# The adapters of the last four batches multiplied together in four column quadrants

## The chip, the cores and the metric

The kernel runs on one core of a Trainium2 chip. The metric is the device time of one execution in microseconds; the figure given for a kernel is the median of several runs. The profile is of one further execution, taken by the hardware profiler, and has its own time.

A core has four engines that matter here, each with its own instruction stream: TensorE multiplies matrices (PE in the profile, PEld for its loads of weights), VectorE (DVE) and ScalarE (ACT) work elementwise, and SyncE (SP) issues nearly all the transfers. TensorE writes to PSUM, which has eight banks of 128 partitions by 512 fp32 numbers.

## The reference

Eight batches of 256 tokens with 1,024 features each go through a low-rank adapter that each batch chooses by its number, then through a feed-forward layer in quantized form, and the result is added to the input. Cut to what matters (one matmul each; `q` rounds to fp8 after division by an input scale):

```
B_sel, A_sel = B[ids], A[ids]              # per batch: 16 x 1024 and 1024 x 16
Bx   = einsum('bni,bri->bnr', x, B_sel)    # "B product", rank 16
c    = einsum('bnr,bor->bno', Bx, A_sel)   # "A product"
gate = q(c) @ gate_w.T ;  up = q(c) @ up_w.T       # 1024 -> 2752
hid  = silu(gate) * up
out  = x + q(hid) @ down_w.T                       # 2752 -> 1024
```

The adapters are applied in fp32, the feed-forward layer takes the fp8 values of its inputs.

## The kernel before, in words

The tokens are transposed on the host, so features lie on partitions and tokens are columns. The 2,048 tokens are four tiles of 512 columns, t = 0 to 3; tile t holds batches 2t and 2t+1 as two halves of 256 columns. The 1,024 features are eight slices of 128, k = 0 to 7. The 2,752 inner features are 22 chunks c of 128 (the last is a half).

**Adapters.** For each t, `load_adapters` reads the two chosen adapters: `b_sel[t]` (128 rows of 136 numbers for each batch: eight slices of 16 columns, and eight scales) and `a_sel[t]` (64 rows for each batch). `spread_b(t)` (L397) copies each 16-column slice of B four times side by side on VectorE (L401), so that a slice is 64 columns wide. `times_b(t)` (L406) multiplies: for each k, one matmul for each of the two batches, 64 columns of weights against 256 columns of x, the first batch into PSUM partitions 0 to 63 and the second into 64 to 127 (L412). Because B stands there four times, the rank-16 result of each batch appears at four places, at partitions 0, 32, 64 and 96, each pair of which belongs to one batch. VectorE copies it to `bm` (L420). `times_a(t)` (L423) then multiplies by A from those four places at once, each a matmul with 16 rows, for different output slices (L430): two halves of eight matmuls, each into four PSUM banks `c`, which ScalarE and VectorE in turn round to fp8 into `xg[t]` (L446, L442).

**Gate and up.** `gate_up(c, t)` (L449) multiplies one chunk of weights by one tile: eight matmuls of 128x128 by 512 columns into y0 (gate) and eight into y1 (up) (L457), in the order of slices `ORDER`, in which `times_a` gets them ready. ScalarE applies silu to y0 (L470), VectorE multiplies by y1 into `hid` (L471). For some (c, t), ScalarE also runs notes (L384, L391): passes over weights, `xg` and `hid` that sum up low bits and squares, from which the kernel decides at its end whether its fast path was allowed.

**Down.** For each output slice, 22 matmuls for each tile (L553), then VectorE adds x (L561), and the result is written out.

**Order.** The order of work is written out by hand at L493 to L516, TensorE follows it. Tile 0's adapter comes first. Then, for t = 1, 2, 3: the B product of tile t, chunk 0 of tile t-1 (for t > 1), chunk 1 of tile t-1, in whose middle (between y0 and y1) stands the A product of tile t. After tile 3: chunks 0 and 1 of it, then chunks 2 to 21 over all tiles. PSUM is one pool of eight banks that all of these take in turn.

**Transfers.** SyncE issues them in program order: x and adapters of tile 0, weights of chunk 0, adapters and x of tile 1, chunk 1, adapters and x of tile 2, the same of tile 3, and then chunk 2 and on. Weights have five buffers, so chunks 0 to 4 are loaded without waiting for a buffer; the load of a later chunk waits until a former one has been multiplied and noted. The transfers take turns on eight completion semaphores, so that each also waits for the landing of the eighth transfer before it. An adapter's place in memory comes from a register that SyncE loads from the list of numbers (L307).

Of the kernel before, what the change touches and what calls it, by code (L numbers as in the profile page):

```python
# [8 lines left out]
F32 = mybir.dt.float32  # L9
# [4 lines left out]
AF = mybir.ActivationFunctionType  # L14
ALU = mybir.AluOpType
AX = mybir.AxisListType

P = 128
T = 2048
SEQ = 256  # L20
NB = 8
H = 1024
I = 2752
R = 16
NH = H // P
NI = (I + P - 1) // P
TAIL = I - (NI - 1) * P
TB = 512
NTB = T // TB
HALF = NI // 2  # L30

ORDER = [0, 1, 4, 5, 2, 3, 6, 7]
# [4 lines left out]
GATE_IN, GATE_W, UP_IN, UP_W, DOWN_IN, DOWN_W = range(6)  # L37
# [214 lines left out]
def adaln_ffn(  # L252
# [13 lines left out]
    nc = tc.nc  # L266
    const = ctx.enter_context(tc.tile_pool(name="const", bufs=1))
    psum = ctx.enter_context(
        tc.tile_pool(name="psum", bufs=8, space=bass.MemoryType.PSUM)
    )  # L270


    ids_i = const.tile([1, NB], I32, name="ids_i")
# [13 lines left out]
    with ExitStack() as fast:  # L287
        acts = fast.enter_context(tc.tile_pool(name="acts", bufs=1))
        lora = fast.enter_context(tc.tile_pool(name="lora", bufs=1))
# [4 lines left out]
        xs = [acts.tile([P, NH, TB], F32, name=f"x{t}") for t in range(NTB)]  # L294
        xg = [acts.tile([P, NH, TB], FP8, name=f"xg{t}") for t in range(NTB)]
# [1 line left out]

        b_sel = [lora.tile([P, 2, NH * R + 8], F32, name=f"b_sel{t}") for t in range(NTB)]  # L300
        a_sel = [lora.tile([P, H // 2], F32, name=f"a_sel{t}") for t in range(NTB)]

        def load_adapters(t, *queues):

            for queue in queues:
                ids_t = [
                    queue.value_load(ids_i[0:1, b : b + 1], min_val=0, max_val=7)  # L307
                    for b in (2 * t, 2 * t + 1)
                ]
                for j, i in enumerate(ids_t):  # L310
                    if queue is queues[0]:
                        queue.dma_start(out=b_sel[t][:, j], in_=b8[bass.ds(i * P, P), :])  # L312
                    if queue is queues[-1]:
                        queue.dma_start(
                            out=a_sel[t][64 * j : 64 * (j + 1)],
                            in_=a8[bass.ds(i * 64, 64), :],
                        )

        def load_x(t, first, n):
            ks = slice(first, first + n)  # L320
            nc.sync.dma_start(out=xs[t][:, ks, :], in_=x4[t][:, ks, :])
# [3 lines left out]
        def load_gate_up(c):  # L325
            n = NH if c == NI - 1 else 2 * NH
            w = wpool.tile([P, 2 * NH, P], F32, tag="w", name="w_gu")[:, :n]
            at = c * 2 * NH * P
            nc.sync.dma_start(
                out=w, in_=w_gu[:, at : at + n * P].rearrange("p (k n) -> p k n", n=P)  # L330
            )
            w_of[c] = w
# [3 lines left out]
        load_adapters(0, nc.scalar, nc.sync)  # L336
        load_x(0, 6, 2)
        load_gate_up(0)
        for t in range(1, NTB):
            load_adapters(t, nc.sync)  # L340
            load_x(t, 0, 4)
            load_x(t, 4, 4)
            if t == 1:
                load_gate_up(1)


        sc = b_sel[0][:, 0, NH * R :]
        inv = const.tile([P, 6], F32, name="inv")
# [48 lines left out]
        def spread_b(t):  # L397
            b_pad = lora.tile([P, 2, NH, 4, R], F32, tag="b_pad", name="b_pad", bufs=2)
            for j in range(2):
                b = b_sel[t][:, j, : NH * R].rearrange("p (k o r) -> p k o r", k=NH, o=1)  # L400
                spread = nc.vector.tensor_copy(b_pad[:, j], b.to_broadcast((P, NH, 4, R)))  # L401
                if t:
                    tc.keep_in_program_order(spread)
            return b_pad

        def times_b(t, b_pad):  # L406


            bx = psum.tile([P, SEQ], F32, tag="ps", name="bx")
            for k in range(NH):  # L410
                for j in range(2):
                    nc.tensor.matmul(  # L412
                        bx[64 * j : 64 * (j + 1)],
                        lhsT=b_pad[:, j, k].rearrange("p o r -> p (o r)"),
                        rhs=xs[t][:, k, bass.ts(j, SEQ)],
                        start=(k == 0),
                        stop=(k == NH - 1),
                    )
            bm = lora.tile([P, SEQ], F32, tag="bm", name="bm", bufs=2)
            nc.vector.tensor_copy(bm, bx)  # L420
            return bm

        def times_a(t, bm):  # L423

            for half in range(2):
                cs = [psum.tile([P, 2, SEQ], F32, tag="ps", name=f"c{q}") for q in range(4)]
                for i in range(2):
                    for q in range(4):
                        rows = slice(32 * q, 32 * q + R)
                        nc.tensor.matmul(  # L430
                            cs[q][:, i],
                            lhsT=a_sel[t][rows, bass.ts(2 * half + i, P)],
                            rhs=bm[rows],
                            start=True,
                            stop=True,
                        )
                for q in range(4):
                    k = 4 * (q % 2) + 2 * half
                    to = xg[t][:, k : k + 2, bass.ts(q // 2, SEQ)]
                    scale = inv[:, GATE_IN : GATE_IN + 1]  # L440
                    if q % 2:
                        nc.vector.tensor_scalar(  # L442
                            to, cs[q], scale, None, ALU.mult, saturate=False
                        )
                    else:
                        nc.scalar.activation(to, cs[q], AF.Copy, scale=scale, saturate=False)  # L446


        def gate_up(c, t, between=None):  # L449
            tail = c == NI - 1  # L450
            w = w_of[c]
            cols = bass.ts(t, TB)
            ys = []
            for j in range(1 if tail else 2):
                y = psum.tile([P, TB], F32, tag="ps", name=f"y{j}")
                for k in ORDER:
                    nc.tensor.matmul(  # L457
                        y,
                        lhsT=high(w[:, j * NH + k, :]),
                        rhs=xg[t][:, k, :],  # L460
                        start=(k == ORDER[0]),
                        stop=(k == ORDER[-1]),
                    )
                ys.append(y)
                if between and not j:
                    between()
            gates, ups = (ys[0], ys[-1]) if not tail else (ys[0][:TAIL], ys[0][TAIL:])
            rows = slice(TAIL, P) if tail else slice(0, P)
            g = work.tile([P, TB], F32, tag="g", name="g")
            nc.scalar.activation(g[rows], gates, AF.Silu, scale=gate_s[: gates.shape[0]])  # L470
            nc.vector.scalar_tensor_tensor(  # L471
                hid[c][rows, cols],
                in0=ups,
                scalar=up_by_down[rows],
                in1=g[rows],
                op0=ALU.mult,
                op1=ALU.mult,
                saturate=False,
            )
            if t == 1 and c > 1:  # L480
                for done in {2: (0, 2), 3: (1, 3)}.get(c, (c,)):
                    note_low_bits(w_of[done], P, done)
                if c <= 1 + 2 * NTB:
                    i, half = divmod(c - 2, 2)
                    ks = slice(half * NH // 2, (half + 1) * NH // 2)
                    note_squares(xg[i][:, ks, :], P, c - 2)
                for done in (0, 1) if c == 2 else (c - 1,):
                    note_squares(hid[done], P, 2 * NTB + done)
# [9 lines left out]
        b_pad = spread_b(0)  # L498
        times_a(0, times_b(0, b_pad))
        b_pad = spread_b(1)  # L500
        gate_up(0, 0)
        for t in range(1, NTB):
            bm = times_b(t, b_pad)
            if t > 1:
                gate_up(0, t - 1)
            if t + 1 < NTB:
                b_pad = spread_b(t + 1)
            gate_up(1, t - 1, between=lambda: times_a(t, bm))
        gate_up(0, NTB - 1)
        gate_up(1, NTB - 1)  # L510
        for c in range(2, NI):
            load_gate_up(c)
            if c == NI - 2:
                nc.sync.dma_start(out=wt[TAIL:], in_=w_d_tail)
            for t in range(NTB):
                gate_up(c, t)  # L516
# [20 lines left out]
        for k in range(NH):  # L537
# [10 lines left out]
            for t in range(NTB):  # L548
                cols = bass.ts(t, TB)
                y = psum.tile([P, TB], F32, tag="ps", name="yd")  # L550
                for c in range(NI):
# [3 lines left out]
                        lhsT=high(wt[:, k, :] if tail else ws[c]),  # L555
                        rhs=hid[c][:, cols],
                        start=(c == 0),
                        stop=tail,
# [9 lines left out]
    with tc.If(others > 0):  # L568
        general(
            tc, psum, x4, aT, bT, w_gu, w_d, w_d_tail, outT, ids,  # L570
            inv=inv, gate_s=gate_s, up_by_down=up_by_down, down_s=down_s,
# [76 lines left out]
```

## Time and profile before

| | us |
|---|---|
| median of 3 runs | 491.61 |
| lowest, highest | 491.53, 492.59 |
| the profiled execution's own time | 492.39 |
| its span, first to last instruction | 490.5 |
| PE busy | 481.2 |
| ACT busy | 192.1 |
| DVE busy | 106.8 |
| matmuls of the B products (L412), busy in all | 15.0 |
| matmuls of the A products (L430), busy in all | 8.0 |

A line of a group reads: line, engine, operation, what it writes and reads, shapes, how often, then busy time in all and mean nanoseconds of one, and the idle time of the engine just before it with what ended that. Matmuls overlap in the array, so one's length times their number is more than the busy time. In the chain of work that ended last, each piece has its start, its length, engine, tile, line and the number of instructions; in the lines of SyncE, the length is that of issuing, not of the transfer.

### The profile page before, as it was taken

The page shows a single profiled execution, that of the slowest core. Times are in us where ns is not written, and L with a number is a line of the kernel's source. Part 1 is how long each engine was busy: PE and PEld are TensorE (multiplying, and loading weights), DVE is VectorE, ACT ScalarE, POOL GpSimd, SP SyncE. Part 2 cuts the span into 40 slices and gives each one's busy share as a digit, 9 for nine tenths or more (in the row PEclk, how much of TensorE's full clock was granted, in tenths as well). Part 3 has the DMA queues.
Part 4 walks back from the last instruction along what each step waited for, and adds up shares of the span by engine and source line. Part 5 has one row for each costly group of instructions (what it writes and reads, how often), then busy time and mean ns, then how long its engine had stood idle before and what let it go on. Part 6 is the DMA issues. An engine that isn't in the chain of part 4 may idle for free.

```text
span 490.5 us, 5796 instructions
## 1 busy us (share of the span) xinstructions
PE 481.2 (98%) x2416; PEld 226.4 (46%) x2416; DVE 106.8 (22%) x163; ACT 192.1 (39%) x243; POOL 2.9 (1%) x6
## 2 busy tenths in 40 slices
PE   8999999999999999999999999999999999999995
PEld 7455544444444444444444444444444444444442
DVE  1344412222121212222121212132111111112111
ACT  1222358756666554444545454459212112021000
POOL 2000000000000000000000000000000000000000
PEclk9899999999999999999999999999999999999998
DMA  8996014422112222222112111112515425333111
GB/s 290 351 373 255 1 38 142 165 86 87 37 55 80 86 87 86 87 86 84 36 53 86 43 61 53 60 54 82 166 71 160 135 86 176 106 115 119 43 66 49
DMA packets 13284, 52.66 MB, mean 107 GB/s; under 512 B 1538, under 2 KB 2562, under 8 KB 9666
## 3 DMA queue, kind: packets, MB, share of 16 engines
q1 hardware_dynamic: 12960, 52.07, 31.0%
q8 instruction: 21, 0.34, 0.3%
q10 hardware_dynamic: 290, 0.14, 0.1%
q14 instruction: 13, 0.11, 0.1%
HBM read 43.81 MB, written 8.39 MB: 106 GB/s over the span
## 4 chain that ended last, share of the span: by engine, by line
PE 97%; DMA 1%; ACT 0%; DVE 0%; ACTq 0%; issue 0%
PE y L457 61%; PE yd L553 31%; PE bx L412 3%; PE c L430 1%; DMA b_sel<-b 1%; ACT xg L446 0%; ACT L275 0%; DVE o L561 0%; ACTq L307 0%; ACTq L274 0%; DVE bm L420 0%; DVE b_pad L401 0%; DVE inv L349 0%; PE count L531 0%; ACTq L312 0%
## 5 line engine op out<-in xcount | busy, mean ns | idle before, releaser
L457 PE MATMUL y<-xg,w_gu 128*128 128x512 fp8e4 x1376 | 299.9, 381 | 0.5 <-ACT xg L446 0.5
L457 PEld LDWEIGHTS <-w_gu 128*128 128x128 bf16 x1376 | 134.5, 98 | 164.9 <-issue 5.2
L553 PE MATMUL yd<-hid,w_d 128*128 128x512 fp8e4 x672 | 150.3, 379 | 0.0
L470 ACT ACTIVATE g<-y,gate_s 128x512 f32<-128x512 f32 (+1 forms) x88 | 59.8, 681 | 152.4 <-PE y L457 152.4
L471 DVE SCALAR_TENSOR_TENSOR hid<-y,up_by_down,g 128x512 fp8e4<-128x512 f32 (+1 forms) x88 | 66.0, 751 | 226.3 <-PE y L457 157.5
L553 PEld LDWEIGHTS <-w_d 128*128 128x128 bf16 x672 | 65.7, 98 | 79.1
L384 ACT ACTIVATE junk<-w_d 128x1408 bf16<-128x1408 uint16 (+1 forms) x16 | 21.2, 1324 | 89.3 <-DMA w_d<-w_d 89.1
L561 DVE SCALAR_TENSOR_TENSOR o<-yd,down_s,x 128x512 f32<-128x512 f32 x32 | 24.0, 751 | 121.9 <-PE yd L553 121.9
L391 ACT ACTIVATE junk<-hid 128x2048 bf16<-128x2048 fp8e4 x22 | 41.9, 1906 | 0.5
L384 ACT ACTIVATE junk<-w_gu 128x2048 bf16<-128x2048 uint16 (+1 forms) x22 | 41.0, 1863 | 0.1
L412 PE MATMUL bx<-x,b_pad 128*64 128x256 f32 x128 | 15.0, 382 | 1.4 <-DVE b_pad L401 1.4
L391 ACT ACTIVATE junk<-xg 128x2048 bf16<-128x2048 fp8e4 x8 | 15.3, 1907 | 0.2
L446 ACT ACTIVATE xg<-c,inv 128x512 fp8e4<-128x512 f32 x16 | 9.7, 687 | 13.5 <-PE c L430 13.5
L412 PEld LDWEIGHTS bx<-x,b_pad 128*64 128x64 f32 x128 | 10.0, 137 | 6.1 <-DVE b_pad L401 1.7
L442 DVE TENSOR_SCALAR xg<-c,inv 128x512 fp8e4<-128x512 f32 x16 | 10.9, 745 | 6.4 <-PE c L430 6.4
L553 PE MATMUL yd<-hid,w_dt 128*128 128x512 fp8e4 x32 | 12.1, 379 | 0.0
L430 PE MATMUL c<-bm,a_sel 16*128 16x256 f32 x128 | 8.0, 387 | 0.5 <-DVE bm L420 0.5
L495 PE MATMUL warm<-zeros 128*128 128x128 bf16 x78 | 6.9, 277 | 1.0 <-DVE zeros L277 1.0
L430 PEld LDWEIGHTS c<-bm,a_sel 16*128 16x128 f32 x128 | 6.2, 184 | 2.5 <-DVE bm L420 1.0
L495 PEld LDWEIGHTS <-zeros 128*128 128x128 bf16 x78 | 6.8, 130 | 1.0 <-DVE zeros L277 1.0
L553 PEld LDWEIGHTS <-w_dt 128*128 128x128 bf16 x32 | 3.1, 98 | 3.8
L420 DVE COPY bm<-bx 128x256 f32<-128x256 f32 x4 | 1.7, 425 | 12.1 <-PE bx L412 12.1
(31 smaller groups left out, 24.0 us busy)
## 6 DMA issues: line engine op xcount, KB each, us to landing
w_gu<-w_gu SPq DMA_DIRECT2D x21, 1024.0 KB, 4.8
outT<-o SPq DMA_DIRECT2D x32, 256.0 KB, 2.1
x<-x SPq DMA_DIRECT2D x7, 1024.0 KB, 9.8
w_d<-w_d SPq DMA_DIRECT2D x8, 704.0 KB, 4.6
w_d<-w_d SPq DMA_DIRECT2D x8, 640.0 KB, 3.8
x<-x SPq DMA_DIRECT2D x2, 512.0 KB, 6.4
a_sel<-a SPq DMA_DIRECT2D x8, 128.0 KB, 7.0
w_gu<-w_gu SPq DMA_DIRECT2D x1, 512.0 KB
```

The costliest lines, as they stand in the source:

```text
L384: nc.scalar.activation(junk_like(w), low(w), AF.Copy, accum_out=lows[:rows, column : column + 1])
L391: nc.scalar.activation(junk_like(q), q, AF.Square, accum_out=squares[:rows, column : column + 1])
L412: nc.tensor.matmul(bx[64 * j : 64 * (j + 1)], lhsT=b_pad[:, j, k].rearrange("p o r -> p (o r)"), rhs=xs[t][:, k, bass.ts(j, SEQ)], start=( ...
L430: nc.tensor.matmul(cs[q][:, i], lhsT=a_sel[t][rows, bass.ts(2 * half + i, P)], rhs=bm[rows], start=True, stop=True,)
L442: nc.vector.tensor_scalar(to, cs[q], scale, None, ALU.mult, saturate=False)
L446: nc.scalar.activation(to, cs[q], AF.Copy, scale=scale, saturate=False)
L457: nc.tensor.matmul(y, lhsT=high(w[:, j * NH + k, :]), rhs=xg[t][:, k, :], start=(k == ORDER[0]), stop=(k == ORDER[-1]),)
L470: nc.scalar.activation(g[rows], gates, AF.Silu, scale=gate_s[: gates.shape[0]])
L471: nc.vector.scalar_tensor_tensor(hid[c][rows, cols], in0=ups, scalar=up_by_down[rows], in1=g[rows], op0=ALU.mult, op1=ALU.mult, saturate=F ...
L495: nc.tensor.matmul(warm[:, :P], lhsT=zeros, rhs=zeros, start=(i == 0), stop=(i == 77))
L553: nc.tensor.matmul(y, lhsT=high(wt[:, k, :] if tail else ws[c]), rhs=hid[c][:, cols], start=(c == 0), stop=tail,)
L561: nc.vector.scalar_tensor_tensor(o, in0=y, scalar=down_s, in1=xs[t][:, k, :], op0=ALU.mult, op1=ALU.add)
```

## The change

Tiles 0 and 1 stay as they are. For tiles 2 and 3, that is batches 4 to 7:

- `load_four` reads the four adapters, B without copies: `b_four` holds the four batches' B side by side, with 16 zero columns after the last (a memset), and `a_four` the four A, at partitions 0, 32, 64 and 96, 16 rows each, over all 1,024 outputs. It stands after chunk 1's weights in the order of transfers; then come x of tiles 2 and 3, and then chunk 2.
- `four_times_b` multiplies, for each k, all four batches, each with 32 columns of `b_four` (its 16, and the 16 that follow, whose results nobody reads) into its own quadrant of 32 PSUM partitions. `bm` then holds the four batches' results at partitions 0, 32, 64 and 96.
- `four_times_a` multiplies by A, one batch for each quadrant of rows, two output slices at a time.
- The order of work changes: both chunks 0 and 1 of tile 1 are done before the B product of the four, chunk 2 of tile 0 lies around the first half of the A product, chunk 2 of tile 1 after the second half, and then chunks 0, 1 and 2 of tile 2 and of tile 3. From chunk 3 on it is as before. Tiles 2 and 3 take the slices in plain order.
- The notes of chunk 2 move from tile 1 to tile 3.

```diff
+        b_four = lora.tile([P, 4 * (NH * R + 8) + R], F32, name="b_four")
+        nc.vector.memset(b_four[:, 4 * (NH * R + 8) :], 0.0)
+        a_four = lora.tile([P, H], F32, name="a_four")
...
+        def load_four():
+            for q in range(4):
+                i = nc.sync.value_load(ids_i[0:1, 4 + q : 5 + q], min_val=0, max_val=7)
+                nc.sync.dma_start(
+                    out=b_four[:, q * (NH * R + 8) : (q + 1) * (NH * R + 8)],
+                    in_=b8[bass.ds(i * P, P), :],
+                )
+                nc.sync.dma_start(
+                    out=a_four[32 * q : 32 * q + R], in_=aT[bass.ds(i * R, R), :]
+                )
...
-        for t in range(1, NTB):
-            load_adapters(t, nc.sync)
+        load_adapters(1, nc.sync)
+        load_x(1, 0, 4)
+        load_x(1, 4, 4)
+        load_gate_up(1)
+        load_four()
+        for t in (2, 3):
             load_x(t, 0, 4)
             load_x(t, 4, 4)
-            if t == 1:
-                load_gate_up(1)
+        load_gate_up(2)
...
+        def four_times_b():
+
+            bx = psum.tile([P, SEQ], F32, tag="ps", name="bx")
+            for k in range(NH):
+                for q in range(4):
+                    at = q * (NH * R + 8) + k * R
+                    nc.tensor.matmul(
+                        bx[32 * q : 32 * (q + 1)],
+                        lhsT=b_four[:, at : at + 32],
+                        rhs=xs[2 + q // 2][:, k, bass.ts(q % 2, SEQ)],
+                        start=(k == 0),
+                        stop=(k == NH - 1),
+                    )
+            bm = lora.tile([P, SEQ], F32, tag="bm", name="bm", bufs=2)
+            nc.vector.tensor_copy(bm, bx)
+            return bm
+
+        def four_times_a(bm, pairs):
+            for i in pairs:
+                cs = [psum.tile([P, 2, SEQ], F32, tag="ps", name=f"c{q}") for q in range(4)]
+                for k in range(2):
+                    for q in range(4):
+                        rows = slice(32 * q, 32 * q + R)
+                        nc.tensor.matmul(
+                            cs[q][:, k],
+                            lhsT=a_four[rows, bass.ts(2 * i + k, P)],
+                            rhs=bm[rows],
+                            start=True,
+                            stop=True,
+                        )
+                for q in range(4):
+                    to = xg[2 + q // 2][:, 2 * i : 2 * i + 2, bass.ts(q % 2, SEQ)]
+                    round_to(to, cs[q], nc.vector if q % 2 else nc.scalar)
...
-                for k in ORDER:
+                order = ORDER if t < 2 else range(NH)
+                for k in order:
...
-            if t == 1 and c > 1:
+            if c > 1 and t == (NTB - 1 if c == 2 else 1):
...
-        for t in range(1, NTB):
-            bm = times_b(t, b_pad)
-            if t > 1:
-                gate_up(0, t - 1)
-            if t + 1 < NTB:
-                b_pad = spread_b(t + 1)
-            gate_up(1, t - 1, between=lambda: times_a(t, bm))
-        gate_up(0, NTB - 1)
-        gate_up(1, NTB - 1)
-        for c in range(2, NI):
+        bm = times_b(1, b_pad)
+        gate_up(1, 0, between=lambda: times_a(1, bm))
+        gate_up(0, 1)
+        gate_up(1, 1)
+        bm = four_times_b()
+        gate_up(2, 0, between=lambda: four_times_a(bm, (0, 1)))
+        four_times_a(bm, (2, 3))
+        gate_up(2, 1)
+        for t in (2, 3):
+            for c in range(3):
+                gate_up(c, t)
+        for c in range(3, NI):
             load_gate_up(c)
...
```

More of the change, by code (lines that the diff above doesn't have):

```diff
@@ L296, in adaln_ffn @@
         hid = [acts.tile([P, T], FP8, name=f"hid{c}") for c in range(NI)]
-        b_sel = [lora.tile([P, 2, NH * R + 8], F32, name=f"b_sel{t}") for t in range(NTB)]
-        a_sel = [lora.tile([P, H // 2], F32, name=f"a_sel{t}") for t in range(NTB)]
+        b_sel = [lora.tile([P, 2, NH * R + 8], F32, name=f"b_sel{t}") for t in range(2)]
+        a_sel = [lora.tile([P, H // 2], F32, name=f"a_sel{t}") for t in range(2)]
+        b_four = lora.tile([P, 4 * (NH * R + 8) + R], F32, name="b_four")
+        nc.vector.memset(b_four[:, 4 * (NH * R + 8) :], 0.0)
+        a_four = lora.tile([P, H], F32, name="a_four")
         def load_adapters(t, *queues):
@@ L421, in times_b, with round_to @@
             return bm
+        def round_to(to, c, engine):
+            scale = inv[:, GATE_IN : GATE_IN + 1]
+            if engine is nc.vector:
+                nc.vector.tensor_scalar(to, c, scale, None, ALU.mult, saturate=False)
+            else:
+                nc.scalar.activation(to, c, AF.Copy, scale=scale, saturate=False)
         def times_a(t, bm):
@@ L439, in times_a @@
                     to = xg[t][:, k : k + 2, bass.ts(q // 2, SEQ)]
[L440 to L443, printed above, removed]
-                        )
-                    else:
-                        nc.scalar.activation(to, cs[q], AF.Copy, scale=scale, saturate=False)
+                    round_to(to, cs[q], nc.vector if q % 2 else nc.scalar)
[26 more added lines that the diff above has]
+                            stop=True,
+                        )
+                for q in range(4):
+                    to = xg[2 + q // 2][:, 2 * i : 2 * i + 2, bass.ts(q % 2, SEQ)]
+                    round_to(to, cs[q], nc.vector if q % 2 else nc.scalar)
         def gate_up(c, t, between=None):
@@ L460, in gate_up @@
                         rhs=xg[t][:, k, :],
-                        start=(k == ORDER[0]),
-                        stop=(k == ORDER[-1]),
+                        start=(k == order[0]),
+                        stop=(k == order[-1]),
                     )
```

## The prediction

> **What bounds the kernel now.** I read the page's totals and chain first, then its groups, then the chain in order of time, then the waits, and last the queue of SyncE.
>
> Page of the kernel before: span, totals, the chain's shares, three groups.
>
> ```profile
> span 490.5 us, 5796 instructions
> ...
> PE 481.2 (98%) x2416; PEld 226.4 (46%) x2416; DVE 106.8 (22%) x163; ACT 192.1 (39%) x243; POOL 2.9 (1%) x6
> ...
> PE 97%; DMA 1%; ACT 0%; DVE 0%; ACTq 0%; issue 0%
> ...
> L457 PE MATMUL y<-xg,w_gu 128*128 128x512 fp8e4 x1376 | 299.9, 381 | 0.5 <-ACT xg L446 0.5
> ...
> L412 PE MATMUL bx<-x,b_pad 128*64 128x256 f32 x128 | 15.0, 382 | 1.4 <-DVE b_pad L401 1.4
> ...
> L430 PE MATMUL c<-bm,a_sel 16*128 16x256 f32 x128 | 8.0, 387 | 0.5 <-DVE bm L420 0.5
> ```
>
> TensorE is the chain for 97% of the span. So a microsecond taken from its stream after the start comes off the end, if no new wait takes its place. The groups say how the matmuls overlap: each lasts about 380 ns, but y (L457) takes 299.9 / 1376 = 218 ns apiece, bx 15.0 / 128 = 117 ns and c 8.0 / 128 = 62 ns. The trace's single start times give the pattern: y one every 216 ns, bx two 7 ns apart every 216 ns, c four 7 ns apart every 216 ns. I call one such beat a round: bx now runs two wide (two halves of the columns), c four wide (four row quadrants). Each fp32 product stands in the trace as two passes, so the 16 products of one `times_b` are 32 passes, or 16 rounds.
>
> Chain in order of time: start, length, what.
>
> ```profile
> 27.08 1.94 PE c L430 x32
> 29.02 1.83 PE y L457 x8
> 30.85 3.60 PE bx L412 x32
> 34.46 5.29 PE y L457 x24
> 39.74 1.94 PE c L430 x32
> 41.68 1.83 PE y L457 x8
> 43.52 3.60 PE bx L412 x32
> 47.12 5.29 PE y L457 x24
> 52.41 1.94 PE c L430 x32
> 54.35 278.10 PE y L457 x1288
> ```
>
> The adapters of t=1 to 3 lie on the chain bare, between runs of y. No gap stands between the pieces, and TensorE's waits hold only four entries, all before 16.4 us. After that it never waits.
>
> **What the Trainium skill says.** "TensorE: Matmul & The Clock Gate", Part 3 (Measured speedup vs the span model): tiles of the array run together, span about one matmul's length plus 4 ns per further tile, and 16 tiles of 32x32 gave 10.6x, thus four column tiles over each row strip at once. The trace agrees for two column tiles (7 ns apart) and four row tiles; it shows no four column tiles over all 128 rows. "TensorEngine Tiling (Array Packing)", Key Properties: changing the tiling mode drains the engine. The trace prices it: the step into or out of a block is 0.31 us instead of 0.216. "DMA: Bandwidth & Descriptors", How many engines (k): a transfer is split by its outer rows, so 16 rows go to 16 engines; no row shows that here.
>
> **The change, part by part.**
>
> *B products of t=2, 3.* Before, one block costs, from the last y before it to the first y after it less one y beat, 34.389 - 30.473 - 0.216 = 3.70 us, and 0.01 more in the next beat: 3.71. It is made of the step in 0.309, a first round of 0.267, 14 further rounds of 0.216, and the step out 0.312. Two blocks: 7.42. After: `four_times_b` has 32 products = 64 passes, four wide 16 rounds, so the same block once; four weight loads in its first round may make that 0.320, as in c. I take 3.74. Gain 3.68 us. The same number of passes is issued; what goes is 16 rounds and one pair of steps.
> Bounds of the width, which this trace does not show: four wide 3.72 to 3.78; two wide 64/2 = 32 rounds, 3.71 + 16 x 0.216 = 7.17; one at a time 64 rounds, 14.1. I take four wide: c shows that four matmuls with their loads are issued within one beat, bx that loads of different columns over the same rows overlap, and the page named above has four column tiles together.
>
> *A products.* Before two blocks `times_a` (t=2, 3) of 32 passes, (41.615 - 39.364) - 0.216 + 0.01 = 2.05 each. After two blocks `four_times_a` of 32 passes, four row quadrants. Same: 0.
>
> *PSUM under the A products.* Now block, 8 y, block follow at once. Eight banks turn in order. From the row before, with block start = 0: ACT empties its c from 1.16 to 3.58, DVE from 1.20 to 3.93, then hid to 4.70. Block two starts at 3.77 and needs the second to fifth c, free by 3.0. Its last c, at about 4.75, needs the bank of y1, freed by hid at 4.70. I put 0 to 0.15 for that, 0.03 taken.
>
> *Spreading copies and the added memset.* Four copies of 0.42 us (L401, t=2, 3) go, one small memset comes, on DVE, which is 22% busy and idle from 1.1 to 8.4 us: 0. Without that cover the memset would cost what DVE's first ones last, 0.06 to 0.11 us; the copies were hidden too.
>
> *Order of y.* The number of y matmuls is the same. `ORDER` for t=2, 3 becomes plain, since the pairs are emptied in that order. The last part of their xg is written about 4 us after the second A block starts; that block (2 us) and the y of (2,1) (3.45 us) stand before the first reader: 0. Without that cover, the first y of (0,2) would wait up to 2 us.
>
> *DMA.* SyncE issues in program order, and the DMAs take eight semaphores in turn, so each waits for the eighth before it.
>
> ```profile
> 17.14 1.49 SPq L321 DMA_DIRECT2D x<-x  x2
> 20.73 0.34 SPq L312 DMA_DIRECT2D b_sel<-b  x1
> 24.07 0.47 SPq L314 DMA_DIRECT2D a_sel<-a  x1
> ...
> 26.31 0.81 SPq L321 DMA_DIRECT2D x<-x  x2
> 27.93 4.09 SPq L329 DMA_DIRECT2D w_gu<-w_gu  x3
> ```
>
> The a_sel at 24.07 waited for chunk 1's weights (issued 11.36, landed 12.7 later). After, the eight small loads come in a row behind those weights, the eighth waits for the same landing, and all four x loads, chunk 2, 3 and 4 and the tail weights stand behind it on the queue. The four register loads between them (about 0.6 us each in the rows of L307) fall between 16 and 21 us and delay nothing that this wait does not. So x2 is issued at about 24.6 instead of 17.14. With data to fetch again at 24.6, the first landing is an undisturbed 1 MB load away: 4.8 us (page, w_gu), so 29.4. Before, when the queue was full, landings were 2.4 us apart (x3's second half 26.70 + 11.2 = 37.9, chunk 2 27.93 + 12.4 = 40.3, chunk 3 31.22 + 11.5 = 42.7). So x2 is whole at 31.8, x3 at 34.3 and 36.7, chunk 2 at 39.1. All small loads have landed by then; their bytes shrink (a: 64 KB instead of 128).
> Need: y of (0,1) starts at 30.69; 32 y end at 37.60, where `four_times_b` starts; its k=4 at about 39.5; chunk 2 is first read at 37.60 + 3.74 = 41.34. Margins 2.8 us for x3 and 2.2 for chunk 2: 0. Before, chunk 2 wasn't read until about 63 us (54.28 + 40 y of 0.216); that cover is gone. At the bad end, small loads that still run 1.7 us and one slow megabyte (x2's second half took 3.3), chunk 2 lands at 41.7: 0.4 us of stall, and all that follows on TensorE is 0.4 later.
>
> *Notes on ACT.* Low bits and squares of chunk 2 come after (2,3) instead of (2,1): five of 1.9 + 0.2 us, then four for chunk 3 only 7 us later instead of 14. Silu falls up to some 4.5 us behind (9 notes 19 us + 4 x 0.7 against four to six y pairs of 3.45), and a bank is wanted again four pairs, 13.8 us, later: 0. Chunk 5's load, waiting for chunk 0's note, goes from 70.9 to about 74 and lands near 79; it is read at 100.6. Chunks 6 to 8, behind it on the queue, come up to some 6 us closer to their use and are read 13.8 us apart from then on: 0.
>
> Sum: -3.68 + 0.03 = -3.65. The profiled span goes 490.5 to 486.8, its own time 492.39 to 488.7. That execution lies 0.8 above the median of the three runs, 491.61; the gain is rounds of TensorE, so I take it off the median: **488.0 us**.
>
> **Rivals.** *Two wide.* The four quadrants pair up: 7.17 + against 7.42, -0.25 + 0.03, 491.4. For: the trace has no four column tiles on fp32 with 128 rows. Against: the page above, and c's issue rate. *Chunk 2 or x3 late.* A further 1 to 3 us beyond the margins: 489 to 491. For: a queue that holds everything behind the eighth small load. Against: 2.2 us of margin, and the loads are issued within 3 us of each other. *Slower: quadrants one after another.* In `four_times_b` alone: 64 rounds, 14.1 instead of 7.42, 491.6 + 6.7 = 498.3. It decides from 33 rounds on, where the block costs more than the two it replaces. For: weights of 32 columns and the fourth quadrant are not in this trace. Against: bx overlaps its halves fully.
>
> **How the numbers follow.** As forecast 0.82 (own range 487.2 to 488.8: the steps, the PSUM wait, and 0.5 for the spread of runs); late data 0.05; two wide 0.08; one after another 0.05. The first two are faster, two wide is the same (0.2%, 1.0 us, is about what a measurement of this kernel tells from no change), the last is slower. To leave out no more than 2 in 10 the range takes in the stalls up to 1.8 us: 487.2 to 489.8.
>
> **What would show it.** One bx block of t=2, 3 near 3.7 us with 64 passes, four starts within some 20 ns and 216 to the next four; two A blocks of 1.94; no wait of TensorE after 16.4 us. Wrong if the bx block is 7 or 14 us, if TensorE waits for x or w_gu between 37 and 42 us, or if the run of y behind 50 us is broken by a wait for ACT.

## The result, and the profile after

The changed kernel takes 488.78 us (median of six runs, 486.88 to 489.65) where the kernel before takes 491.68 (six runs): a ratio of 0.9933, with a 95% interval of 0.9911 to 0.9956. That is 2.9 us less, between 2.2 and 4.4. The forecast was 488.0, with a range of 487.2 to 489.8.

The page of the changed kernel, in the lines that answer to those of before (the group of the four's B product is too small to stand on the page):

```profile
span 485.1 us, 5786 instructions
...
PE 476.7 (98%) x2416; PEld 224.2 (46%) x2416; DVE 105.1 (22%) x159; ACT 192.0 (40%) x243; POOL 2.9 (1%) x6
...
L512 PE MATMUL y<-xg,w_gu 128*128 128x512 fp8e4 x1376 | 298.2, 379 | 0.8 <-ACT xg L447 0.5
...
L431 PE MATMUL bx<-x,b_pad 128*64 128x256 f32 x64 | 7.7, 382 | 0.3 <-DVE b_pad L420 0.3
```

The span is 5.4 us shorter, more than the medians tell. This execution (486.88) is the quickest of its six, and that of before (492.39) lies above its median. Their starts differ, in work that is the same in both kernels: chunk 0 of tile 0 took 3.84 us here, and began 0.67 us earlier. Before, it took 5.22 us, in a window in which TensorE was granted 0.67 of its clock (PEclk, the third number from the end):

```profile
16.35:21.57 5.22, 5.22 (x16) 1.85 (x16) 2.12 (x5) 1.79 (x3) 0.00 (x0) 0.67 1.01 424
```

So the two profiles are compared from behind that, from the B product of tile 1 on.

TensorE in order of time, the kernel after (start, length, then what it waited for):

```profile
19.52 3.67 PE L431 MATMUL bx<-x,b_pad 128*64 128x256 f32 x32
23.21 1.90 PE L512 MATMUL y<-xg,w_gu 128*128 128x512 fp8e4 x8
...
26.98 8.81 PE L512 MATMUL y<-xg,w_gu 128*128 128x512 fp8e4 x40
35.72 3.66 PE L474 MATMUL bx<-x,b_four 128*32 128x256 f32 x64
39.55 1.90 PE L512 MATMUL y<-xg,w_gu 128*128 128x512 fp8e4 x8 [0.17 <-DMA w_gu<-w_gu]
41.38 2.01 PE L491 MATMUL c<-bm,a_four 16*128 16x256 f32 x32
43.32 1.90 PE L512 MATMUL y<-xg,w_gu 128*128 128x512 fp8e4 x8
45.15 2.11 PE L491 MATMUL c<-bm,a_four 16*128 16x256 f32 x32
```

Sixty-four passes of the B product (L474) take 3.66 us, where 32 take 3.67 (L431 here, L412 before). Two things are less good: the y behind it waits for chunk 2's weights (the row says 0.17; against a step without a wait it is 0.24), and the second A block is 0.1 longer than the first.

The queue of SyncE in the kernel after, with the time of issuing:

```profile
20.14 0.33 SPq L327 DMA_DIRECT2D b_four<-b  x1
23.18 0.33 SPq L331 DMA_DIRECT2D a_four<-aT  x1
23.56 2.34 SPq L337 DMA_DIRECT2D x<-x  x4
25.95 1.52 SPq L345 DMA_DIRECT2D w_gu<-w_gu  x3
```

The eighth small load waits for chunk 1's landing at 23.16, and all the rest stands behind it, as forecast.

**The account.** The table follows TensorE's stream in each profile from the first B pass of tile 1 to a common point, the 1,287th y from the last. A wait is what the step from the last pass of a B product to the first y behind it takes above the 0.312 us that it takes without one. Three profiles are of the kernel before (one here, two in the last experiment), four of the changed kernel.

| profile | tile 1's B starts, us | way from there | wait for chunk 1 | wait for chunk 2 | the rest |
|---|---|---|---|---|---|
| before, first | 21.57 | 32.94 | 0 | 0 | 32.94 |
| before, second and third | 19.56, 20.08 | 33.87, 34.03 | 0.94, 1.09 | 0 | 32.94 |
| after, first | 19.52 | 29.63 | 0.09 | 0.24 | 29.31 |
| after, three more | 20.25, 20.65, 20.80 | 30.53, 29.56, 30.06 | 0.96, 0.08, 0.62 | 0.26, 0.16, 0.13 | 29.31 |

The rest is the same to 0.01 us within each kernel, and 3.63 us apart: two B blocks of 3.71 less one of 3.70, less the 0.10 of the second A block. The forecast sum was 3.65.

### The profile page after: what moved, and what is told of

Its sections match the earlier page's. It is cut to its first block, busy times and chain, and to the rows that moved or that the text cites. A ratio compares the mean times of both kernels' runs of the same rounds, so it can differ in the third digit from the quotient of the medians.

```text
span 485.1 us, 5786 instructions
## 1 busy us (share of the span) xinstructions
PE 476.7 (98%) x2416; PEld 224.2 (46%) x2416; DVE 105.1 (22%) x159; ACT 192.0 (40%) x243; POOL 2.9 (1%) x6
## 4 chain that ended last, share of the span: by engine, by line
PE 91%; DMA 6%; SPq 2%; issue 0%; DVE 0%
PE y L512 58%; PE yd L610 31%; DMA w_gu<-w_gu 5%; PE c L491 1%; SPq L337 1%; SPq L319 0%; SPq L312 0%; DMA ids_i<-ids 0%; SPq L317 0%; DVE o L618 0%; SPq L345 0%; SPq L331 0%; PE count L588 0%
## 5 line engine op out<-in xcount | busy, mean ns | idle before, releaser
L431 PE MATMUL bx<-x,b_pad 128*64 128x256 f32 x64 | 7.7, 382 | 0.3 <-DVE b_pad L420 0.3
L431 PEld LDWEIGHTS bx<-x,b_pad 128*64 128x64 f32 x64 | 5.5, 137 | 2.1 <-DVE b_pad L420 0.5
L456 PE MATMUL c<-bm,a_sel 16*128 16x256 f32 x64 | 4.0, 387 | 0.5 <-DVE bm L439 0.5
L403 ACT ACTIVATION_READ_ACCUMULATOR junk<-w_gu 128x1 f32 x22 | 4.2, 192 | 0.0
L410 ACT ACTIVATION_READ_ACCUMULATOR junk<-hid 128x1 f32 x22 | 4.1, 188 | 0.0
```

The source lines that it names most:

```text
L403: nc.scalar.activation(junk_like(w), low(w), AF.Copy, accum_out=lows[:rows, column : column + 1])
L410: nc.scalar.activation(junk_like(q), q, AF.Square, accum_out=squares[:rows, column : column + 1])
L431: nc.tensor.matmul(bx[64 * j : 64 * (j + 1)], lhsT=b_pad[:, j, k].rearrange("p o r -> p (o r)"), rhs=xs[t][:, k, bass.ts(j, SEQ)], start=( ...
```

## The experiments

**Is it the width?** Two kernels with the same 64 passes in another order: one quadrant after the other, and two pairs, the second after the first.

```diff
-            for k in range(NH):
-                for q in range(4):
+            for q in range(4):
+                for k in range(NH):
```
```diff
-            for k in range(NH):
-                for q in range(4):
+            for k, q in [(k, p + j) for p in (0, 2) for k in range(NH) for j in range(2)]:
+                if True:
```

> The four quadrants of the B product one after another: the quadrant is the outer loop, the slice the inner one; the same 64 passes. If the width makes the gain: 64 rounds instead of 16, the bx block 14.1 us instead of 3.7, the time 10.4 us above the changed kernel, about 499. If the gain lies in the new order of work or in fewer steps between modes, the time stays within 1 us of the changed kernel's 488.8.

> The four quadrants as two pairs, the second pair after the first; the same 64 passes. If the width makes the gain: 32 rounds, the bx block 7.2 us, the time 3.45 us above the changed kernel, 492.2, thus within 1 us of the kernel before: the new order of work without the width is worth nothing. If the new order brings something of its own: 490 or less.

A third keeps the new order of work and takes back the old products:

```diff
...
-        load_four()
+        load_adapters(2, nc.sync)
+        load_adapters(3, nc.sync)
...
+        b_pads = [spread_b(t) for t in (2, 3)]
         gate_up(0, 1)
         gate_up(1, 1)
-        bm = four_times_b()
-        gate_up(2, 0, between=lambda: four_times_a(bm, (0, 1)))
-        four_times_a(bm, (2, 3))
+        bms = [times_b(t, b) for t, b in zip((2, 3), b_pads)]
+        gate_up(2, 0, between=lambda: times_a(2, bms[0]))
+        times_a(3, bms[1])
```

> The new order of work alone: tiles 2 and 3 keep their copies of B and their own B and A products, in the place of the four. If the width makes the gain, this is two blocks of 16 rounds in one, 6.5 to 7.2 us, which saves one pair of steps and perhaps some rounds at the handover: 0.2 to 0.9 us below the kernel before. If the order of work makes it: 3 us below.

Measured: one by one 496.62 us (two runs), 7.9 above the changed kernel on the same chip; two wide 491.35, ratio to before 0.9982 (0.9973 to 0.9990); the order alone 492.16 against 492.04, ratio 1.0001 (0.9991 to 1.0011). So the new order of work brings nothing that a measurement can tell, and the width brings the gain. The block itself, TensorE in order of time, in the three kernels:

```profile
37.55 11.50 PE L474 MATMUL bx<-x,b_four 128*32 128x256 f32 x64
```
```profile
38.00 6.27 PE L474 MATMUL bx<-x,b_four 128*32 128x256 f32 x64
```
```profile
38.20 7.13 PE L429 MATMUL bx<-x,b_pad 128*64 128x256 f32 x64
```

Two sizes were missed. The order alone was to be 0.2 to 0.9 us below before: its block saves 0.26 of 7.42, the second A block gives back 0.10, and the rest is below what a run tells. And the first two blocks are shorter than rounds of 0.216 us make them. From first to last start, 63 rounds would be 13.6 us and the trace has 11.12; 31 would be 6.7 and it has 5.90. The starts of single passes show where that comes from. In the two-wide kernel the 13th pair starts 2.614 and 2.621 us after the first pass; two more passes start at 2.626 and 2.633, and from there four start in each beat until the first pair is through. The records don't name the quadrant. But two passes of one quadrant stand 0.216 us or more apart everywhere else, and the weight loads of the two passes at 2.626 and 2.633 carry waits for the second pair's own transfers. So these are the first passes of the second pair: they stand 27th and 28th in time, where the program has them 33rd and 34th. Where the columns are the same for both tiles (the order alone) nothing overlaps: 6.75.

**How near is chunk 2?** In the changed kernel chunk 2 lands 16.3 us after chunk 1 (23.16 and 39.50 in its first profile), and TensorE wants it 16.10 us after it begins with chunk 1. The loads of chunks 2 and 3 changed places:

```diff
+        load_gate_up(3)
         load_gate_up(2)
...
         for c in range(3, NI):
-            load_gate_up(c)
+            if c > 3:
+                load_gate_up(c)
```

> The loads of chunks 2 and 3 change places, so that chunk 2 lands one megabyte (2.5 us) later; nothing else. Theory, a margin of nearly nothing: in the changed kernel chunk 2 lands 16.35 us after chunk 1, and TensorE wants it 16.10 us after it begins with chunk 1; so where TensorE waited for chunk 1 it waits for chunk 2 by about 2.7 us here, and 1.2 us or more otherwise; the time is 1.3 to 2.6 us above the changed kernel's, 490.0 to 491.3. Rival, the margin of 2.2 us that was forecast: 0 to 0.5 us above.

Measured: 491.38 us, 2.5 above the changed kernel on the same chip (488.90), a little over the top of the theory's span; its nine runs go from 490.85 to 492.88. Its TensorE in order of time, then the window with the granted clock:

```profile
43.33 3.44 PE L513 MATMUL y<-xg,w_gu 128*128 128x512 fp8e4 x8 [2.50 <-DMA w_gu<-w_gu]
```
```profile
43.30:46.70 3.40, 3.37 (x9) 1.02 (x9) 0.00 (x0) 0.00 (x0) 0.00 (x0) 0.53 0.68 199
```

The wait is 2.50 us in the row and 2.56 against a step without one, near the 2.7 that the theory gave for an execution that also waits for chunk 1, as this one does; there is no reserve of 2.2 us. On top of it, the clock fell to 0.53 behind the wait, and eight y took 2.80 us between first and last start instead of 1.52. With the A block behind them, which started late as well, this second price is 1.6 us (the rest of the account is 30.94 here and 29.31 in the changed kernel). It was not expected.

The nine runs lie in two groups: five from 490.85 to 491.38, with mean granted clocks of 0.995 to 0.997, and four from 492.44 to 492.88, three of them with 0.989 to 0.993 and one with 0.996. The profiled run (492.66, 0.993) is of the upper group. It fits this that the lower group escaped the second price, but only one run has a profile, so it is not shown.

**Can the lull be taken out?** While the queue stands behind the eighth small load, the transfers of the changed kernel run low (131 and 185 GB/s between 22 and 26 us, below). Here the loads of tile 2's x go ahead of the small ones; `load_four` is split in two, and the loads of A go behind chunk 2:

```diff
-        load_four()
-        for t in (2, 3):
-            load_x(t, 0, 4)
-            load_x(t, 4, 4)
+        load_x(2, 0, 4)
+        load_x(2, 4, 4)
+        load_b_four()
+        load_x(3, 0, 4)
+        load_x(3, 4, 4)
         load_gate_up(2)
+        load_a_four()
```

> Only the order of the loads is changed: x of tile 2, then the four small loads of B, x of tile 3, chunk 2, the four small loads of A, chunk 3. If the eighth small load's wait for chunk 1 leaves the transfers idle for a time and so makes chunk 2 late: x2 is issued 6 us earlier, chunk 2 lands about 2 us earlier than in the changed kernel's profile (near 37.5 instead of 39.5), TensorE waits for no w_gu, and the median is 0.2 to 1.0 us below the changed kernel's. If the spread of the changed kernel's runs comes from their starts alone, the two are the same within 0.5 us.

> The changed kernel itself, unaltered, once more beside the kernel before. If the gain is 16 rounds of TensorE (3.65 us) and chunk 2's weights cost nothing in most runs, the difference of the medians is 3.2 to 4.0 us. If chunk 2's weights come late in most runs, it is 2.0 to 3.2 us, and the profile shows TensorE waiting for w_gu after the bx block by 0.2 us or more.

> The kernel with x of tile 2 ahead of the small loads once more, beside the changed kernel on the same chip. If its gain of 0.6 us was real: 0.3 to 0.9 us below the changed kernel, chunk 1 landing within 2.6 us of x1 instead of 3.0 to 3.4, and no wait for w_gu before chunk 2. If it was the starts' luck: within 0.2 us.

> The changed kernel once more, as the other side of that comparison. 3.0 to 3.6 us below the kernel before (3.68 less 0.1 for a bank and 0 to 0.25 for chunk 2).

Measured: 488.07 us against 488.71 for the changed kernel on one chip, 487.80 against 488.90 on another, with four runs of this order each time; ratios to the kernel before 0.9910 (0.9895 to 0.9926) and 0.9906 (0.9892 to 0.9921), where the changed kernel has 0.9927 (0.9914 to 0.9941) and 0.9931 (0.9914 to 0.9949). Both times this order is ahead, the second time by more than was expected, but the intervals overlap. The changed kernel itself lies 3.3 and 3.1 us below the kernel before. The 3.3 is in the range that was expected if chunk 2 costs nothing, and yet its profile has a wait of 0.26 for chunk 2; the medians are too coarse to tell the two cases apart.

The transfers in windows of 2 us (last number: GB/s), the changed kernel (first profile) and then the other order (second profile):

```profile
22.00:24.00 2.00, 1.98 (x16) 0.92 (x13) 0.43 (x1) 0.00 (x0) 0.00 (x0) 1.00 0.76 131
24.00:26.00 2.00, 2.00 (x22) 1.22 (x23) 0.00 (x0) 0.69 (x1) 0.00 (x0) 1.00 0.74 185
```
```profile
22.00:24.00 2.00, 2.00 (x18) 1.07 (x15) 0.25 (x1) 0.00 (x0) 0.00 (x0) 1.00 1.02 430
24.00:26.00 2.00, 2.00 (x16) 1.01 (x17) 0.18 (x1) 0.42 (x1) 0.00 (x0) 1.00 1.00 422
```

And TensorE of the other order at chunk 2, without a wait:

```profile
36.15 3.66 PE L480 MATMUL bx<-x,b_four 128*32 128x256 f32 x64
39.74 1.90 PE L518 MATMUL y<-xg,w_gu 128*128 128x512 fp8e4 x8
```

The lull is gone. Chunk 2 lands at 38.4 in the first profile, 14.6 us after chunk 1 instead of 16.3 (not at 37.5, but in time), and neither profile of this order has a wait for it; the rest of their way is 29.33 in both. Chunk 1 also lands sooner after tile 1's x: 2.46 and 2.47 us behind its second half, where all profiles with small loads next in the queue have 3.04 to 3.52. Something goes again at the end: from VectorE's last output to the end of the span, the three profiles with this order of loads (the third follows) have 5.8 to 5.9 us, the other eleven 5.0 to 5.4. Why, no run shows.

**The second A block, and the spread.** In this order of loads, the second half of the A product was put between gate and up of the next tile:

```diff
-        four_times_a(bm, (2, 3))
-        gate_up(2, 1)
+        gate_up(2, 1, between=lambda: four_times_a(bm, (2, 3)))
```

> The order of loads with x of tile 2 first, and the second half of the four's A product moved from before chunk 2 of tile 1 to between that chunk's gate and up. If the 0.1 us that this block takes longer than the first comes from the bank of the up part, which VectorE has still to empty: both blocks take the same (1.94 to 1.97 us), and the time is 0.1 us below the kernel with that order of loads, 487.7 to 487.9. If it comes from something else, the second block keeps its 2.04.

> The changed kernel a third time, to see its runs beside those of the other order of loads. If its runs fall apart into two groups by chance of the start, some lie near 488 and some near 489.6; the other order's stay below 488.2 if it removes more than a wait of 0.25 us for chunk 2, and reach 489 if it does not.

Its chain in order of time:

```profile
42.23 1.96 PE c L497 x32
44.19 3.56 PE y L518 x16
47.75 1.94 PE c L497 x32
```

The block is back at 1.94 and the rest at 29.23 instead of 29.33: the 0.1 us was the wait for the bank of the up part. The time doesn't show it: 488.35 us, 0.3 below the changed kernel beside it (488.68), and above the 488.07 and 487.80 that the order of loads alone had on other chips. One of its runs is at 489.68, so the idea that this order keeps the runs below 488.2 fell. The changed kernel's six lie from 488.42 to 488.89 but for one at 490.41; in two earlier sets of six they lay in two groups, near 488 and near 489.6 (486.88 to 488.22 and 489.34 to 489.65; 487.68 to 488.32 and 489.47 to 489.82). What parts them stays open. Over all runs, 14 with this order of loads have a median of 488.06, 23 of the changed kernel 488.71.

**Does the kernel before wait for chunk 1 too?**

> The kernel before, unaltered, for a second profile: in the first its start was slow (chunk 0 of tile 0 at 0.67 of the clock), and TensorE came to chunk 1 after the weights had landed. If a quick start is lost at chunk 1 in both kernels alike: with chunk 0 of tile 0 in 3.84 us, TensorE waits for w_gu at chunk 1 by 0.1 to 1.0 us here too, and from there on the way to the last adapter's end is 32.6 us without that wait, 3.6 longer than in the changed kernel. If the wait at chunk 1 is the change's doing: none here.

> The same once more, since the start varies from run to run: as for the other look at the kernel before.

Measured 491.47 and 492.12 us, both with a quick start, both with the wait. The row in the waits of TensorE, in the first and in the second of them:

```profile
PE y L457 <- DMA w_gu<-w_gu: 0.9, 1, 0.9
```
```profile
PE y L457 <- DMA w_gu<-w_gu: 1.0, 1, 1.0
```

So a quick start is taken back at chunk 1 in both kernels: its landing, not TensorE, sets the time there. This is no doing of the change.

## Why the prediction was right, point by point

- **B products, -3.68: right.** Four wide, 16 rounds, four starts 7 ns apart and 216 ns to the next four, as forecast; first round 0.240 instead of 0.32, so the block costs 3.70 without the wait (from the last y before it to the first behind it 4.138, less 0.235, less one beat of 0.216, and 0.01) and not 3.74. The rivals *two wide* and *one after another* are out for the kernel as it is; their prices, made real by the order of the passes, were less than forecast, since a free quadrant starts early. Two sums are slightly off as written: with 0.320 for the first round the block would be 3.76, not 3.74, and *one after another* would lose from 34 rounds on, not from 33, which cost 3.71 + 17 x 0.216 = 7.38, still under 7.42.
- **A products 0, bank 0.03 of 0 to 0.15: the place right, the size 0.10.** The last c of the second block waits for the bank of y1, as worked out. That the sum of 3.65 came so near to 3.63 is in part luck: the block was 0.04 better than forecast and the bank 0.07 worse.
- **DMA 0, with a margin of 2.2 us for chunk 2: this step failed in size.** By the forecast's own sign (TensorE waits for w_gu between 37 and 42 us) it was wrong. Two terms were off. One is the landings: "the first landing is an undisturbed 1 MB load away: 4.8 us" was 5.5 (issue 23.56, landing 29.02), and x2's second half took 3.1 more instead of 2.4, so chunk 2 came 16.3 us after chunk 1 and not 15.0. The other is the need: 41.34 was read from an execution with a slow start, in which TensorE began with chunk 1 at 25.18, 1.1 us after it had landed. With a quick start TensorE begins with chunk 1 as it lands and wants chunk 2 16.10 us later. A stall, which the forecast had at its bad end only (0.4), was the usual case: 0.13 to 0.26 in four profiles. The margin of x3 shrank too: its second half landed 0.4 to 0.6 us before its first use, not 2.8. The rival *chunk 2 late* thus holds in its mechanism, far below its 1 us; the range, which took in stalls up to 1.8 us, covered it.
- **Notes on ACT, order of y, chunk 5's load: right.** Behind 47.2 us the y run of 1,296 is unbroken; chunk 5 was issued at 72.5 (forecast about 74).
- **Off the median.** The account gives 3.63 less 0.13 to 0.26, about 3.4; the four comparisons of medians gave 2.9, 3.3, 3.1 and 3.1. Each interval reaches 3.4, but all four lie below. What the remaining 0.3 is, if it is anything, stays open; the starts differ by more than that from run to run.

## What to carry to other kernels

Here the fp32 products of 32 columns cost least with all four column quadrants filled at once, and the beat can be read from the starts of single matmuls: the saving is the number of beats, whatever the number of passes. Before moving work that needs a later load forward, count the distance between landings against the distance between needs, from the last wait that both kernels share, and not from the clock of one execution. A small transfer that has to wait for a completion holds back every large one behind it on its queue; with the large ones first, the lull in the transfers and the wait for chunk 2 were gone.

## What the runs showed of the hardware

- Matmuls of a column quadrant that is free start ahead of earlier ones in the program whose quadrant is taken, as the starts and waits of two traces have it: six passes early in the two-wide kernel, some four beats at each of three handovers in the one by one. The Trainium skill, "TensorE: Matmul & The Clock Gate", Part 3 (The mechanism), says that matmuls are never reordered, in start or end; these two traces show starts out of program order.
- One wait of 2.5 us was followed by eight matmuls at 0.53 of the clock (one profile), while waits of 0.9 to 1.1 us at the same kind of step were not followed by any loss.
- With small loads (64 to 128 KB each) next in the queue, a 1 MB load landed 3.04 to 3.52 us after the one before it (eleven profiles); with large ones next, 2.46 or 2.47 (three).
